# Statistics groups, measuring lead, residual images and opening of a normalise-and-convolve kernel

## The chip, the cores and the metric

One core of a Trainium2 chip. The metric is the device time of the whole program in microseconds, as the median of several runs. The engines are PE (TensorE), DVE (VectorE), ACT (ScalarE), POOL (GpSimd) and SP (SyncE, which here issues DMAs).

## What is computed

160 images of 128 channels and 32x32 pixels are group-normalised (32 groups of 4 channels), convolved with one of five quantised 3x3 weight sets, and added to the input.

```python
def _L0_conv_ref(x, U):
    beta = jnp.max(U); alpha = jnp.min(U)
    s1 = (beta - alpha) / 3.0
    v1 = s1 * _ste_floor(U / s1)
    s2 = s1 / 5.0
    v2 = s2 * _ste_floor((U - v1) / s2)
    w = (v1 + v2).reshape(OUT_CH * N, IN_CH, K, K)
    xb = x.reshape(B // N, N * C, H, W)
    act = jax.lax.conv_general_dilated(xb, w, (1, 1), [(1, 1), (1, 1)], feature_group_count=N)
    return act.reshape(B, C, H, W)
...
x = x + _L0_conv_ref(_gn(x), L0_conv_U)    # _gn: mean and variance over 4 channels and 32x32 pixels
```

The quantisation steps s1 and s2 come from the range of all five weight sets, so no weight is ready before all of U has been read.

## The kernel before

Images are taken set by set, 32 to each of the five weight sets, one image (128 channels on the partitions, 1024 pixels) at a time; they are loaded in pairs. The order of instructions on every engine is written out by hand in `Main.run`: each engine works through its own queue in the order in which the Python code issues, and waits on semaphores.

*Opening* (lines 782 to 899). SP loads the weight sets: the first two in two halves each, the third, image 0, the last two, then image 1 and further images. DVE takes the maximum and the minimum of each piece (`weight_range`, lines 429 and 430). Images 0 and 1 are measured on ACT meanwhile. PE transposes the range across partitions (`over_partitions`, line 443); the matmul for the means of group 0 is issued between this and the matmul that spreads the result (line 448). DVE works out s1, s2, their reciprocals and split parts on 128x1 tiles (`Steps.from_range`), interleaved with the first operations of the first weight column. `lift` is s2 times a constant, and POOL's scales need it (line 241). A weight set is made in three columns of taps (`COLS` = 1, 0, 2), each in some thirteen 128x384 operations on DVE (`quantise`, `floor_div`), turned on PE (line 472) and kept by ACT and POOL (`keep_column`). Idle stretches of PE are filled with `warm_up` matmuls on zeros (line 649). The first three images are convolved directly, column by column.

*Statistics.* An image is measured by two passes on ACT (line 194 for the sum, 201 for the squares) or, for the images in `BY_VECTOR`, by `bn_stats` on DVE (line 184). Images form groups; when all of a group are measured, its statistics take a chain: means on PE (line 210), a copy on ACT (219), four small operations on POOL (221 to 224, tile dv), variances on PE (227), one operation on ACT (233), and `rstd`, `shift`, `twice` on POOL (237 to 246). Means and variances of a group are issued in two successive iterations, within the convs (`on_the_way`).

*The loop* (from line 902), one iteration per image i. PE does `conv(i)`: first the sums of pairs of rows for image i+1 on the bank m (`sums_of_pairs`), then the rest of image i on eo. From image 7 on, odd images are `combined` (differences and sums of rows are formed in float32 by POOL in `outer_rows`, lines 554 and 555, and by DVE in `combine`, then split into vh by ACT, line 576, and vl by DVE, line 582); even ones are normalised by ACT (523, 531) and DVE forms the low part and its row combinations (589, 603 to 606). From image 146 on two of three images are combined. DVE joins the pairs (lines 735 and 737), which frees the bank m; ACT copies one half of it first (725). The operations for the next weight set are taken one at a time out of a generator (`later`), from the fifth image of the first set and the third of the others to the 29th.

*The lead.* Iteration i measures all images below i + min(10 + i//4, 15). So in the iterations 4, 8, 12, 16 and 20 two images are measured, in others one.

*The result.* The scaled sum is either made by ACT (line 754) and added to the image by an accumulating DMA from POOL (773), or, for images that are `by_hand`, added by DVE in one operation (765). In the main part these are i % 8 == 7 from 31 to 151.

Of the kernel before, what the change touches and what calls it, by code (L numbers as in the profile page):

```python
# [33 lines left out]
class Steps:  # L34
# [15 lines left out]
    def from_range(self, extg):  # L50


        nc, col = self.nc, self.col

        def divide_exact(tag, q1, a, m):

            q0, rem = col(tag + "q0"), col(tag + "rem")
            yield nc.vector.tensor_scalar_mul(q0, a, 1.0 / m)
            yield nc.vector.scalar_tensor_tensor(rem, q0, -(m - 1.0), a, ALU.mult, ALU.add)
            yield nc.vector.tensor_sub(rem, rem, q0)  # L60
            yield nc.vector.scalar_tensor_tensor(q1, rem, 1.0 / m, q0, ALU.mult, ALU.add)

        def parts(out, s):

            r, neg, hi, lo = out
            yield nc.vector.tensor_scalar_mul(neg, s, -1.0)
            yield nc.vector.reciprocal(r, s)
            yield nc.vector.tensor_single_scalar(
                hi.bitcast(I32), neg.bitcast(I32), -4096, op=ALU.bitwise_and
            )  # L70
            yield nc.vector.tensor_sub(lo, neg, hi)

        span = col("span")
        yield nc.vector.tensor_reduce(span, extg, AX.X, ALU.add)
        yield from divide_exact("s1", self.s1, span, 3.0)

        of_s1, s2 = parts(self.parts1, self.s1), divide_exact("s2", self.s2, self.s1, 5.0)
        for chain in (s2, of_s1, of_s1, s2, of_s1, s2, s2, of_s1):
            yield next(chain)
        yield nc.vector.tensor_scalar_mul(self.lift, self.s2, LIFT)  # L80
        yield from parts(self.parts2, self.s2)
        self.span, self.big = span, col("big")
        yield nc.vector.tensor_reduce(self.big, extg, AX.X, ALU.max)
# [51 lines left out]
def run(steps):  # L135

    while True:
        try:
            next(steps)
        except StopIteration as end:  # L140
            return end.value
# [170 lines left out]
class Main:  # L312
# [24 lines left out]
    STAT_LEAD = 14  # L337
    LOAD_LEAD = 18
    STEADY = 7
    BY_VECTOR = (8, 10, 11, 14, 19, 24, 29, 34)  # L340
    THIRDS = 146
    EARLY = 8
    FIRST = 3
# [5 lines left out]
    def __init__(self, tc, ctx, keep, x, u, out):  # L349
        nc = self.nc = tc.nc  # L350
        self.imgs, C, self.H, self.W = x.shape
        P = self.P = nc.NUM_PARTITIONS
        assert C == P and self.H * self.W == 1024
        self.per_set = self.imgs // N_SETS
        self.xv = x.rearrange("(b n) c h w -> n c b (h w)", n=N_SETS)
        self.ov = out.rearrange("(b n) c h w -> n c b (h w)", n=N_SETS)
        self.uv = u.rearrange("n (o i k) -> n o i k", o=C, k=TAPS)

        def pool(name, bufs, **kw):
            return ctx.enter_context(tc.tile_pool(name=name, bufs=bufs, **kw))  # L360

        self.const = pool("const", 1)
        self.qpool = pool("quant", 1)
        self.wpool = pool("weights", 2)
        self.upool = pool("u", 1)
        self.xpool = pool("x", 11)
        self.zpool = pool("z", 3)
        self.parts = pool("parts", 5)
        self.rows = pool("rows", 4)
        self.wide = pool("wide", 2)  # L370
        self.wide_parts = pool("wide_parts", 3)
        self.evac = pool("evac", 2)
        self.sums = pool("sums", 3)
        self.unread = pool("unread", 1)
        self.small = pool("small", 3)
        self.ps_eo = pool("ps_eo", 2, space=PSUM)
        ps_m = pool("ps_m", 1, space=PSUM)
        self.ps_stat = pool("ps_stat", 1, space=PSUM)
        self.ps_tr = pool("ps_tr", 1, space=PSUM)
        self.steps = Steps(nc, keep)  # L380

        self.pair = [
            ps_m.tile([P, self.H // 2, self.W], F32, tag=name, name=name) for name in ("m1", "m2")
        ]
        self.chunks, self.z, self.hi, self.v, self.eo, self.m2 = {}, {}, {}, {}, {}, {}
        self.sum = {}
        self.wts = {}
        self.columns = []

        cuts = [0, 2, 4, 8, 12, 16, 20, *range(24, self.imgs + 1, 8)]  # L390
        self.groups = [range(a, b) for a, b in zip(cuts, cuts[1:])]
        self.group_of = {i: k for k, g in enumerate(self.groups) for i in g}
        self.stats = {}
# [28 lines left out]
    def weight_range(self, us):  # L422

        nc, P = self.nc, self.P
        halved = [part for u in us[:2] for part in (u[:, : P // 2], u[:, P // 2 :])]
        pieces = [*halved, *us[2:]]
        ext = self.const.tile([P, 2, len(pieces)], F32, tag="ext", name="ext")
        for k, piece in enumerate(pieces):
            nc.vector.tensor_reduce(ext[:, 0, k : k + 1], piece, AX.XY, ALU.max)
            nc.vector.tensor_reduce(  # L430
                ext[:, 1, k : k + 1], piece, AX.XY, ALU.min, negate=True
            )
        ext1 = self.const.tile([P, 2], F32, tag="ext1", name="ext1")
        nc.vector.tensor_reduce(ext1, ext, AX.X, ALU.max)
        return ext1

    def over_partitions(self, ext1, ident, between):


        nc, P = self.nc, self.P  # L440
        rows = self.ps_tr.tile([1, 2, P], F32, tag="pt", name="rows")
        for k in range(2):
            nc.tensor.transpose(rows[:, k, :], ext1[:, k : k + 1], ident)
        between()
        top = self.const.tile([1, 2], F32, tag="top", name="top")
        nc.vector.tensor_reduce(top, rows, AX.X, ALU.max)
        spread = self.ps_tr.tile([P, 2], F32, tag="pt", name="spread")
        nc.tensor.matmul(spread, self.ones, top, start=True, stop=True)
        return spread
# [44 lines left out]
    def by_vector(self, i):  # L494
        return i in self.BY_VECTOR

    def stats_of(self, k):
        if k not in self.stats:
            self.stats[k] = Statistics(
                self.nc, self.small, self.ps_stat, self.gavg, self.mhalf, len(self.groups[k]),  # L500
                self.steps.lift, k,
            )
        return self.stats[k]

    def measure(self, i, stages=(0, 1)):


        k = self.group_of[i]
        g = self.groups[k]
        st, j, image = self.stats_of(k), i - g.start, self.image(i)  # L510
        if self.by_vector(i):
            st.image(j, image)
            return
        for s in stages:
            junk = self.unread.tile([self.P, 1024], MM, tag="junk", name=f"junk{i}_{s}")
            (st.image_sum, st.image_square)[s](j, image, junk)
# [222 lines left out]
    def by_hand(self, i):  # L739


        if i < self.FIRST or i >= self.imgs - LAST:
            return True
        return i > self.BY_VECTOR[-1] - 4 and i % 8 == 7

    def residual(self, i):

# [34 lines left out]
    def run(self):  # L782
# [4 lines left out]
        for n in range(N_SETS):  # L787
            if n == 0:
                un = self.upool.tile([P, P, TAPS], F32, tag="u", name="u0")
            else:  # L790
                un = self.space(f"range{n}").rearrange("p j e -> p (j e)")[:, : P * TAPS]
                un = un.rearrange("p (i k) -> p i k", k=TAPS)
            half = P // 2 if n < 2 else P
            for c in range(0, P, half):
                nc.sync.dma_start(un[:, c : c + half], self.uv[n][:, c : c + half])
            self.us[n] = un
            if n == 2:
                self.chunks[0] = self.space("xt0")
                nc.sync.dma_start(self.chunks[0][:, 0, :], self.xv[0, :, 0, :])
        nc.sync.dma_start(self.chunks[0][:, 1, :], self.xv[0, :, 1, :])  # L800
        for c in range(1, 6):
            self.load(c, single=c < 2)
        warm = self.const.tile([P, 1], F32, tag="warm", name="warm")
        nc.vector.memset(warm, 0.0)
# [16 lines left out]

        self.ones = self.const.tile([1, P], F32, tag="ones", name="ones")
        nc.vector.memset(self.ones, 1.0)
        ext1 = self.weight_range(list(self.us.values()))
        for i in range(2):
            self.measure(i)
        spread = self.over_partitions(ext1, ident, self.stats_of(0).means)

        def take(steps, count):
            for _ in range(count):  # L830
# [13 lines left out]
        first, second, third = (  # L844
            self.make_column(0, col, by_scalar=col != self.COLS[0]) for col in self.COLS
        )
        for ahead in (11, 2, 1, 1, 1, 1, 1, 1):
            take(chain, ahead)
            take(first, 1)
        run(chain)  # L850
        self.stats[0].deviations()
        measure(0, 2, 3)
        self.stats[0].variances()
        self.stats[0].deviation()
        measure(1, 2)
        self.stats[0].scales()
        take(second, 1)
        measure(1, 3)
        self.stats[1].means()
        self.stats[1].deviations()  # L860
        self.warm_up(14)
        parts(0)
        self.stats[1].variances()
        self.warm_up(8)
        self.stats[1].deviation()
        self.stats[1].scales()
        parts(1)
        run(first)
        self.warm_up(2)
        parts(2)  # L870
        take(second, 2)
        self.low_part(0)
# [29 lines left out]
        for i in range(self.imgs):  # L902
# [27 lines left out]
            else:  # L930
                j = i - 1
                self.conv(i, on_the_way)
            ahead = i + min(10 + i // 4, self.STAT_LEAD + 1)
            to_measure = range(measured, min(self.imgs, ahead))
            measured += len(to_measure)
            if n + 1 < N_SETS:
# [136 lines left out]
```

## Time and profile before

| | us |
|---|---|
| median of 3 runs | 992.03 (991.75 to 992.63) |
| the profiled execution | 991.75 |
| its span, first to last instruction | 989.9 |
| PE busy | 958.1 (97%) |
| DVE busy | 927.7 (94%) |
| ACT busy | 895.0 (90%) |
| POOL busy | 383.7 (39%) |

In the profile's rows an instruction stands with its line in the kernel, its engine, what it writes and reads (tile names without buffer numbers), its shape, and how often it occurs; in a timeline the first column is its start, the second its duration, and a note in brackets tells how long its engine was idle before it and what ended that. PE's matmuls overlap, so a row of 0.38 us is followed by the next after 0.2 us. The granted clock of PE was 0.999 over the span.

### The profile page before, as it was taken

Reading aid. Unit: us, or ns where it says so; the run is one execution under the profiler, and the core shown is the slowest. Engines: PE = TensorE matmul, PEld = TensorE weight load, DVE = VectorE, ACT = ScalarE, POOL = GpSimd, SP = SyncE. Lnnn points to the kernel's source line nnn. Section 1 sums busy time; section 2 is a strip of 40 time slices with the busy share of each in tenths; the row PEclk is TensorE's granted clock in tenths of the full one; section 3 lists DMA queues with packets and bytes.
Section 4 is the critical chain, followed back from the end, with each engine's and each line's share of the span. In section 5 each row is a group of like instructions: output and inputs, shape, how many; then the busy total and the mean of one; then the engine's idle time right before and its main releaser. Section 6 shows DMA issues by size and latency. Waiting matters only on the chain.

```text
span 989.9 us, 16124 instructions
## 1 busy us (share of the span) xinstructions
PE 958.1 (97%) x5938; PEld 578.4 (58%) x5938; DVE 927.7 (94%) x1256; ACT 895.0 (90%) x1224; POOL 383.7 (39%) x565
## 2 busy tenths in 40 slices
PE   2899999999999999999999999999999999999997
PEld 1445655566656666666655666656665666666564
DVE  7999999999999999999999999999999998889995
ACT  5779999899999999999999999999999999998651
POOL 4324563644316253414263443315243424132410
PEclk9999999999999999999999999999999999999999
DMA  9538999999997999899989999997999898987764
GB/s 358 210 107 239 239 241 272 269 265 274 256 306 178 301 249 293 238 278 246 271 217 269 274 279 237 281 283 220 241 278 304 214 301 215 293 229 205 180 178 153
DMA packets 65129, 246.05 MB, mean 249 GB/s; under 512 B 5008, under 2 KB 5008, under 8 KB 65040
## 3 DMA queue, kind: packets, MB, share of 16 engines
q1 hardware_dynamic: 45312, 173.09, 50.2%
q0 software_dynamic: 19728, 71.84, 37.6%
q8 instruction: 48, 0.79, 0.3%
q14 instruction: 41, 0.34, 0.1%
HBM read 89.19 MB, written 83.89 MB: 175 GB/s over the span
## 4 chain that ended last, share of the span: by engine, by line
PE 72%; DVE 13%; ACT 8%; issue 4%; POOL 2%; DMA 0%; DVEq 0%; ACTq 0%; POOLq 0%
PE eo L668 24%; PE m L668 24%; PE eo L629 23%; ACT vh L576 2%; ACT junk L201 2%; ACT sum L754 2%; DVE eo L735 1%; DVE eo L737 1%; DVE v L565 1%; DVE lo L589 1%; POOL v L554 1%; DVE vl L582 1%; ACT m L725 1%; DVE v L568 1%; DVE v L571 1%
## 5 line engine op out<-in xcount | busy, mean ns | idle before, releaser
L668 PEld LDWEIGHTS <-wt 128*128 128x128 f16 x4266 | 417.2, 98 | 234.6 <-issue 6.0
L629 PE MATMUL eo<-hi,wt 128*128 128x496 f16 (+3 forms) x1422 | 339.6, 375 | 1.4 <-ACT wt L485 0.9
L773 POOL DMA_DIRECT2D xt<-sum x137 | 122.4, 899 | 463.6 <-ACT sum L754 448.9
L629 PEld LDWEIGHTS <-wt 128*128 128x128 f16 x1494 | 146.0, 99 | 141.9 <-ACT wt L485 2.3
L582 DVE SCALAR_TENSOR_TENSOR vl<-v,rstd,vh 128x2048 f16<-128x2048 f32 x80 | 188.2, 2353 | 4.1 <-ACT vh L576 4.1
L668 PE MATMUL m<-vh,wt 128*128 128x496 f16 (+1 forms) x480 | 182.2, 380 | 1.8 <-DVE eo L737 1.1
L668 PE MATMUL eo<-vh,wt 128*128 128x248 f16 (+1 forms) x960 | 183.9, 273 | 0.0
L668 PE MATMUL eo<-vl,wt 128*128 128x248 f16 (+1 forms) x960 | 183.9, 273 | 0.0
L668 PE MATMUL m<-vl,wt 128*128 128x496 f16 (+1 forms) x480 | 182.2, 380 | 0.2 <-DVE vl L582 0.2
L194 ACT ACTIVATE junk<-xt 128x1024 f16<-128x1024 f32 x152 | 160.6, 1057 | 15.5 <-DMA xt<-in_x_dram 12.0
L201 ACT ACTIVATE junk<-xt,mv 128x1024 f16<-128x1024 f32 x152 | 173.8, 1144 | 0.1
L576 ACT ACTIVATE vh<-v,rstd 128x2048 f16<-128x2048 f32 x80 | 160.8, 2010 | 2.5 <-POOL v L555 2.0
L754 ACT ACTIVATE sum<-eo 128x1024 f32<-128x1024 f32 x137 | 138.0, 1008 | 15.4 <-PE eo L668 15.3
L735 DVE TENSOR_TENSOR eo<-m,m 128x512 f32<-128x512 f32 x157 | 109.3, 696 | 36.1 <-ACT m L725 29.0
L668 PE MATMUL eo<-rows,wt 128*128 128x256 f16 (+1 forms) x924 | 138.9, 273 | 0.0
L668 PE MATMUL m<-rows,wt 128*128 128x496 f16 (+1 forms) x462 | 113.4, 380 | 0.4
L737 DVE TENSOR_TENSOR eo<-m,m 128x512 f32<-128x512 f32 x157 | 109.5, 697 | 3.6
L725 ACT COPY m<-m 128x512 f32<-128x512 f32 x157 | 90.5, 577 | 18.4 <-PE m L668 18.4
L523 ACT ACTIVATE z<-xt,shift,rstd 128x1024 f32<-128x1024 f32 x80 | 99.8, 1248 | 2.6 <-POOL shift L244 2.6
L589 DVE TENSOR_TENSOR lo<-z,hi 128x1024 f16<-128x1024 f32 x80 | 98.1, 1226 | 0.0
L565 DVE TENSOR_TENSOR v<-xt 128x960 f32<-128x960 f32 x80 | 92.0, 1149 | 0.0
L531 ACT CAST hi<-z 128x1024 f16<-128x1024 f32 x80 | 83.6, 1045 | 2.5
(111 smaller groups left out, 888.1 us busy)
## 6 DMA issues: line engine op xcount, KB each, us to landing
xt<-in_x_dram SPq DMA_DIRECT2D x78, 1024.0 KB, 9.4
out_dram<-xt SPq DMA_DIRECT2D x78, 1024.0 KB, 5.9
xt<-sum POOLq DMA_DIRECT2D x137, 512.0 KB, 6.1
u<-in_L_conv_U_dram SPq DMA_DIRECT2D x4, 576.0 KB, 9.4
xt<-in_x_dram SPq DMA_DIRECT2D x4, 512.0 KB, 9.7
range<-in_L_conv_U_dram SPq DMA_DIRECT2D x3, 576.0 KB, 7.7
out_dram<-xt SPq DMA_DIRECT2D x3, 512.0 KB, 2.8
u<-in_L_conv_U_dram SPq DMA_DIRECT2D x2, 288.0 KB, 3.0
```

The lines of the kernel that those rows point to most:

```text
L194: self.nc.scalar.activation(junk, image, ACTF.Copy, scale=-1.0 / image.shape[1], accum_out=self.mv[:, j, 0:1],)
L201: self.nc.scalar.activation(junk, image, ACTF.Square, bias=self.mv[:, j, 0:1], accum_out=self.mv[:, j, 1:2],)
L565: nc.vector.tensor_sub(v[:, W:last], x[:, : last - W], x[:, 2 * W :])
L576: self.nc.scalar.mul(vh, self.v[i], st.rstd[:, j])
L582: self.nc.vector.scalar_tensor_tensor(vl, self.v[i], st.rstd[:, j], self.hi[i], ALU.mult, ALU.subtract)
L589: self.nc.vector.tensor_sub(lo[:, 1 : self.H + 1, :].rearrange("p h w -> p (h w)"), self.z.pop(i), self.hi[i].rearrange("p h w -> p (h w)"),)
L629: nc.tensor.matmul(self.bank(target, h)[:, r0 - h0 : r1 - h0, c0:c1], self.wts[n, col][:, k, :], tile[:, s0 : s0 + r1 - r0, c0 + dw : c1 + ...
L668: self.nc.tensor.matmul(target[:, :, c0:c1], self.wts[n, col][:, kind, :], source[:, :, c0 + dw : c1 + dw], start=start, stop=stop, skip_g ...
L735: nc.vector.tensor_add(rows[:, :, 0], m1, m2)
L737: nc.vector.tensor_sub(rows[:, :, 1], m1, m2)
L754: nc.scalar.mul(self.sum[i], eo.rearrange("p h r w -> p (h r w)"), 0.5)
L773: self.nc.gpsimd.dma_start(self.image(i), self.sum.pop(i), accum_op=ALU.add)
```

## The change

Five things are changed.

- Groups of statistics: after 0-1 and 2-3, groups of four images up to image 40 (before: up to image 24), and of eight from there.
- The lead of measuring is min(10 + i//8, 15). Two images are measured in iterations 8, 16, 24, 32 and 40.
- `BY_VECTOR` holds 8, 10, 11, 18, 27, 36, 45, 54 instead of 8, 10, 11, 14, 19, 24, 29, 34.
- `by_hand` in the main part takes i % 8 == 3 from 27 to 139, fifteen images, instead of sixteen with i % 8 == 7 from 31 to 151.
- The opening: only the first weight set is loaded and reduced in halves; all weights are loaded ahead of image 0; images 0 and 1 are measured, and the means of group 0 formed, after the range and the chain of steps; s1's parts come ahead of s2; the first column's operations are interleaved with the small ones in another ratio; 14 and 7 warm-up matmuls instead of 14, 8 and 2; the second column's first pass on ACT comes before the squares of image 2, and `high_part(1)` behind the keeping of the first column.

```diff
-        of_s1, s2 = parts(self.parts1, self.s1), divide_exact("s2", self.s2, self.s1, 5.0)
-        for chain in (s2, of_s1, of_s1, s2, of_s1, s2, s2, of_s1):
-            yield next(chain)
+        yield from parts(self.parts1, self.s1)
+        yield from divide_exact("s2", self.s2, self.s1, 5.0)
...
-    BY_VECTOR = (8, 10, 11, 14, 19, 24, 29, 34)
+    BY_VECTOR = (8, 10, 11, 18, 27, 36, 45, 54)
...
-        cuts = [0, 2, 4, 8, 12, 16, 20, *range(24, self.imgs + 1, 8)]
+        cuts = [0, 2, *range(4, 40, 4), *range(40, self.imgs + 1, 8)]
...
-        halved = [part for u in us[:2] for part in (u[:, : P // 2], u[:, P // 2 :])]
-        pieces = [*halved, *us[2:]]
+        pieces = [us[0][:, : P // 2], us[0][:, P // 2 :], *us[1:]]
...
             nc.tensor.transpose(rows[:, k, :], ext1[:, k : k + 1], ident)
-        between()
...
-        return i > self.BY_VECTOR[-1] - 4 and i % 8 == 7
+        return 24 < i < self.imgs - 20 and i % 8 == 3
...
-            half = P // 2 if n < 2 else P
+            half = P // 2 if n == 0 else P
             for c in range(0, P, half):
                 nc.sync.dma_start(un[:, c : c + half], self.uv[n][:, c : c + half])
             self.us[n] = un
-            if n == 2:
-                self.chunks[0] = self.space("xt0")
-                nc.sync.dma_start(self.chunks[0][:, 0, :], self.xv[0, :, 0, :])
-        nc.sync.dma_start(self.chunks[0][:, 1, :], self.xv[0, :, 1, :])
-        for c in range(1, 6):
+        for c in range(6):
             self.load(c, single=c < 2)
...
-        ext1 = self.weight_range(list(self.us.values()))
-        for i in range(2):
-            self.measure(i)
-        spread = self.over_partitions(ext1, ident, self.stats_of(0).means)
+        spread = self.over_partitions(self.weight_range(list(self.us.values())), ident)
...
-        for ahead in (11, 2, 1, 1, 1, 1, 1, 1):
+        for ahead in (8, 1, 1, 1, 1, 1, 3, 1, 1, 1):
             take(chain, ahead)
             take(first, 1)
         run(chain)
+        measure(0, 0, 1)
+        measure(1, 0, 1)
+        self.stats[0].means()
         self.stats[0].deviations()
         measure(0, 2, 3)
         self.stats[0].variances()
         self.stats[0].deviation()
+        take(second, 1)
         measure(1, 2)
         self.stats[0].scales()
-        take(second, 1)
         measure(1, 3)
         self.stats[1].means()
         self.stats[1].deviations()
         self.warm_up(14)
         parts(0)
         self.stats[1].variances()
-        self.warm_up(8)
         self.stats[1].deviation()
         self.stats[1].scales()
-        parts(1)
+        self.normalise(1)
         run(first)
-        self.warm_up(2)
+        self.warm_up(7)
+        self.high_part(1)
         parts(2)
...
-            ahead = i + min(10 + i // 4, self.STAT_LEAD + 1)
+            ahead = i + min(10 + i // 8, self.STAT_LEAD + 1)
```

More of the change, by code (lines that the diff above doesn't have):

```diff
@@ L435, in weight_range, with over_partitions @@
         return ext1
-    def over_partitions(self, ext1, ident, between):
+    def over_partitions(self, ext1, ident):
         nc, P = self.nc, self.P
@@ L495, in by_vector @@
         return i in self.BY_VECTOR
[L497 to L503, printed above, removed]
     def measure(self, i, stages=(0, 1)):
@@ L509, in measure @@
         g = self.groups[k]
-        st, j, image = self.stats_of(k), i - g.start, self.image(i)
+        if k not in self.stats:
+            self.stats[k] = Statistics(
+                self.nc, self.small, self.ps_stat, self.gavg, self.mhalf, len(g),
+                self.steps.lift, k,
+            )
+        st, j, image = self.stats[k], i - g.start, self.image(i)
         if self.by_vector(i):
```

## The prediction

> **What bounds the kernel now.** I read the busy times by stage first, then who waited for whom on PE, then the order of time where PE stood still. Columns of the stages: start and end, length, then busy time (instructions) of PE, PE's weight loads, DVE, ACT, POOL, the granted clock, the DMA share and GB/s.
>
> ```profile
> 0.00:57.00 57.00, 35.12 (x165) 17.10 (x166) 49.56 (x100) 36.75 (x61) 24.52 (x54) 1.00 0.64 247
> 57.00:135.00 78.00, 76.75 (x464) 44.59 (x463) 76.36 (x118) 71.73 (x102) 38.10 (x53) 1.00 0.83 224
> 135.00:234.00 99.00, 97.09 (x604) 58.40 (x603) 94.97 (x133) 95.55 (x134) 49.27 (x62) 1.00 0.98 262
> 234.00:890.00 656.00, 655.87 (x4105) 399.17 (x4104) 621.40 (x814) 635.35 (x871) 246.99 (x360) 1.00 0.93 260
> 890.00:990.00 100.00, 93.27 (x609) 59.19 (x606) 85.47 (x95) 55.60 (x60) 24.85 (x38) 0.99 0.65 180
> ```
>
> From 234 us (image 32 on) PE is busy 655.87 of 656 us: nothing off PE matters there unless it makes PE wait. Before that PE waits; so the change can act in three places: the opening (to 57 us), images 4 to 31 (to 234 us), and the last images.
>
> PE's rate is read from the order of time: a conv begins with its first matmul on m. Undisturbed, a conv of an odd image takes 3.92 us and one of an even image 7.72 (236.21 to 243.93, 243.93 to 247.85). A conv with a group's means or variances in it takes 0.14 more (7.86, 4.06), one that turns a weight column 0.17 more (4.09). Against this the convs of images 14, 18, 23, 24, 25, 29 and 30 are too long by 0.87, 0.71, 0.63, 0.73, 0.26, 0.32 and 0.36 us, 3.9 in all; between 234 and 890 us only three or four by some 0.2; conv 148 by 0.58. Two of them:
>
> ```profile
> 128.99 2.29 POOL L223 TENSOR_TENSOR dv<-dv 128x4 f32<-128x4 f32 x1
> ...
> 131.35 1.90 POOL L224 TENSOR_TENSOR dv<-dv,mv 128x4 f32<-128x4 f32 x1
> ...
> 133.31 0.39 PE L227 MATMUL pg<-dv,gavg 128*128 128x4 f32 x2 [0.61 <-POOL dv L224]
> ```
> ```profile
> 151.91 0.38 PE L668 MATMUL m<-vl,wt 128*128 128x496 f16 x1
> ...
> 152.10 0.68 DVE L737 TENSOR_TENSOR eo<-m,m 128x512 f32<-128x512 f32 x1
> ...
> 152.84 0.38 PE L668 MATMUL m<-vh,wt 128*128 128x512 f16 x1 [0.55 <-DVE eo L737]
> ```
>
> In the first, POOL's chain for a group's variances is late; in the second DVE is late in freeing the bank m. DVE has 97% busy time there and hardly a gap.
>
> The opening is a chain through DVE. It reduces the weights as they land; PE waits for the range, later for the second column:
>
> ```profile
> 7.60 0.75 DVE L429 TENSOR_REDUCE ext<-range 128x1 f32<-128x576 f32 x1
> 8.26 0.75 DVE L430 TENSOR_REDUCE ext<-range 128x1 f32<-128x576 f32 x1
> 8.92 1.35 DVE L429 TENSOR_REDUCE ext<-range 128x1 f32<-128x1152 f32 x1
> ```
> ```profile
> PE rows L443 <- DVE ext L434: 16.9, 1, 16.9
> ...
> PE pt L472 <- DVE k L114: 1.5, 1, 1.5
> ```
>
> **The change, part by part.**
>
> *Second weight set in one transfer, image 0 behind all weights.* DVE reaches the second set at 6.28 us. Its two halves land 4.5 to 5.1 us after their issue at 1.72 and 2.18, so at 6.2 and 7.2. As one transfer it lands at about 7.2, DVE waits 0.9, and two reduces of a whole set (pitch 1.26 each) replace four of a half (0.66): -0.12. The range is ready 0.75 later. Bounds: -0.12 (the one transfer is there at 6.3) to +0.9. I take 0.75. The third set is needed at 9.8 then and lands by 8.7: no second wait.
>
> *Chains of s1 and s2 no longer interleaved.* Before, eleven small operations come ahead of the first large one, now eight; independent ones cost some 0.07 us, dependent ones 0.2, so the first large one starts 0.17 sooner; three more small ones (about 0.1 each) fall between the large ones: +0.13.
>
> *First images measured behind the range.* Images 0 and 1 need four ACT passes of 1.06 to 1.15 us. Image 1 lands at 14.0 as before (the bytes ahead of it are the same), so ACT ends at 17.7, where before it ended at 16.56; but the means matmul now stands behind the spread on PE, 18.0+0.75+0.58, and ngm moves from 17.75 to 19.8. The lift, which POOL's scales wait for, comes after s2, which is now spread between large operations: 21.24 becomes about 24.2. z0 moves from 23.21 to 25.4. PE's 14 warm-up matmuls (0.43 each) begin 2 us later too, and group 1's variances stand behind them: from 26.03 to about 28.5; ve, z, and the keeping of the first column on ACT follow: the first real matmul moves from 29.38 to about 30.9. What hides part of it: PE stands 1.5 us for the second column (k at 38.33) and ACT 3.25 us. Six passes over three images later PE is free at 38.5 instead of 37.0, and k comes at 38.69+0.88 = 39.6. So the second column is set by DVE's chain again, with 0.3 to 1 us of cover left. DVE's own lo's (31.62, 34.12, later by 0.9) need hi 1 and 2, which I get at 32.3 and 34.6: just in time, and 0.3 is lost if they are not. Opening: **+1.1** (0.1 to 1.9). PE is the bound afterwards, so it reaches the end undiminished. Three fewer warm-ups (0.2 each) lie in waits: 0.
>
> *Groups of four to image 40.* 26 groups instead of 24. Each has two matmul pairs at 0.14: 2 x 0.28 = **+0.56** on PE. ACT gets two copies (0.17) and POOL eight small operations more for each. POOL's price is uncertain:
>
> ```profile
> L223 POOL TENSOR_TENSOR dv<-dv x7: 198/198/2287, 65.2 to 253.3; 128x4 f32<-128x4 f32 x4, 128x8 f32<-128x8 f32 x3
> L224 POOL TENSOR_TENSOR dv<-dv,mv x7: 198/203/1899, 65.6 to 253.6; 128x4 f32<-128x4 f32 x4, 128x8 f32<-128x8 f32 x3
> ```
>
> (shortest, median and longest ns). Of the five group chains in convs 6 to 27 one was slow and cost PE 0.87; with two more chains I take 2 x 0.87/5 = **+0.35**, bounds 0 and two whole stalls, 1.74.
>
> The Trainium skill ("SBUF — State Buffer", "Who interferes with whom") says that DVE and GpSimd share one pair of ports as an exclusive lock, so that the later one blocks for the other's whole instruction. The spread of 198 to 2287 ns agrees. Taken strictly it speaks against more POOL chains where DVE has no gaps: both new chains late would be +1.74 instead of +0.35, and the sum 1.4 us higher.
>
> *Lead grows every 8th image; images by vector.* In both kernels an iteration in which two images are measured has one of them on DVE, so ACT's share per iteration stays at one. Those iterations were 4, 8, 12, 16, 20 (images 14, 19, 24, 29, 34) and are 8, 16, 24, 32, 40 (18, 27, 36, 45, 54). An image costs DVE 1.69 us (121.68 to 123.37). So DVE has 1.7 us less behind it from iteration 4 on, 3.4 from 12, 5.1 from 20, and gets them back at 24, 32 and 40. Of the stalls I take the two where PE waits for DVE (0.71 and 0.73) as gone, the two of POOL and ACT (0.87, 0.63) as halved, since these engines are late partly behind DVE, and the last three (0.94) as left: **-2.2**, bounds -3.9 and 0. The 1.69 us at iterations 32 and 40 fall where DVE is busy 95%, and spread over eight images at 5.87 us: I take +0.2, bounds 0 and 1.4 (two stalls like conv 18's).
>
> *Residual on DVE.* It takes DVE 1.22 us and spares ACT a pass of 1.0. It was at images 31, 39, ... 151, sixteen; now 27, 35, ... 139, fifteen. The iterations that carry it move by four against the groups' ends. In the steady part DVE has 5% and ACT 3% free, and I take 0, with -0.4 (the 0.2 stalls vanish) and +2.6 (0.2 at each of 13) as bounds. At the end images 143 and 151 leave DVE for ACT, which is idle there (55.6 of 100 us): conv 148's wait for vl goes, **-0.5**, bounds -0.6 and 0.
>
> Sum: +1.1 +0.56 +0.35 -2.2 +0.2 -0.5 = -0.5. The profiled execution took 991.75 us (span 989.9), the median of the three runs is 0.28 higher. -0.5 gives 991.25, or **991.5** as a median.
>
> **Rivals.**
> *POOL takes DVE's place (slower).* In convs 15, 18, 22, 26 and 29 the four-image chains meet a DVE without gaps and each keeps PE 0.87; the late scales hold up outer_rows and vh, so the old stalls don't shrink either: 1.1+0.56+4.35-0.5 = +5.5 at worst, 997.5; with three of the five late and half the DVE gain, 1.1+0.56+2.6-1.1-0.5 = +2.7, 994.7. It decides from two late chains on. For it: 5.4 us of POOL at 114.57 and 5.3 at 176.15. Against: four of five chains were quick although DVE was busier.
> *The new phase of the residual collides* with the weight steps, 0.2 at each of 13 images on top of the forecast: -0.5+2.6 = +2.1, 994.1. For it: the stages around 340 us have DVE at 29.8 of 30; against: the parity stays.
> *All early stalls go*: 1.1+0.56-3.9-0.6 = -2.8, 989.2. For it: POOL and ACT wait behind DVE; against: convs 29 and 30 lie where DVE gets work back.
> *The second transfer is hidden anyway* and the opening costs 0.1: -1.5, 990.5.
>
> **How the numbers follow.** A change of 0.2%, 2 us, is about what this measurement tells from none. Forecast 0.52, POOL 0.15, phase 0.11, all stalls gone 0.13, transfer hidden 0.09. The forecast's own range, from half the opening's and the stalls' bounds, is 990.0 to 993.5. Faster by over 0.2% is most of "all stalls gone" and little else: 0.12. Slower is POOL, half of the phase and a tail of the forecast: 0.23. The rest, 0.65, is within. The range of 8 in 10 goes from 989.4 to 994.6.
>
> **What would show it.** Right: PE's first wait 17.6 instead of 16.9 with a DVE wait for the second set before it; the first real matmul near 30.9; conv 4 begins about 1.1 later; convs 18 and 24 without a wait; conv 148 at 7.72. Wrong: PE waiting for POOL's dv or ACT's ve in more than one conv; repeated waits at iterations 28, 36, 44 and so on; an opening that moves by more than 1.9, which would mean that PE or ACT, not DVE, sets the second column.

## The result, and the profile after

The changed kernel takes 995.38 us (median of 6 runs, 994.74 to 996.70) against 991.97 for the kernel before: a ratio of 1.0037, 95% interval 1.0024 to 1.0050. It is slower by 3.4 us; the prediction was 991.5, with a range up to 994.6.

The stages of the changed kernel, with columns as before (start and end, length, busy time of PE, PE's weight loads, DVE, ACT, POOL, clock, DMA share, GB/s); the boundary at 234 us is kept so that the rows compare, and conv 32 begins at 236.2 us before and at 237.8 here:

```profile
0.00:57.00 57.00, 33.72 (x161) 16.40 (x162) 49.03 (x98) 36.67 (x61) 27.14 (x54) 1.00 0.64 247
57.00:135.00 78.00, 77.06 (x466) 44.84 (x465) 73.36 (x108) 72.00 (x102) 43.21 (x50) 1.00 0.83 224
135.00:234.00 99.00, 96.22 (x603) 57.99 (x601) 95.38 (x135) 93.87 (x135) 65.83 (x79) 1.00 0.92 255
234.00:310.00 76.00, 74.75 (x473) 45.67 (x470) 72.14 (x101) 72.26 (x98) 30.57 (x39) 1.00 0.96 258
310.00:893.00 583.00, 583.00 (x3647) 354.65 (x3645) 552.65 (x725) 567.07 (x776) 212.59 (x323) 1.00 0.94 261
```

Between 57 and 135 us DVE has 3 us less to do (73.36 against 76.36), and PE is busy for only 0.3 us more (77.06 against 76.75). From 234 to 310 us PE now stands idle for 1.25 us, where before it had no gap. Who PE waited for between 57 and 900 us (total, times, longest), before and after:

```profile
PE m L668 <- DVE eo L737: 1.1, 2, 0.6
PE pg L227 <- POOL dv L224: 0.6, 1, 0.6
PE eo L629 <- DVE eo L737: 0.5, 1, 0.5
PE m L668 <- ACT m L725: 0.5, 1, 0.5
```
```profile
PE m L660 <- DVE eo L729: 2.2, 6, 0.4
PE m L660 <- DVE vl L574: 1.0, 2, 0.7
PE pt L467 <- DVE m L458: 0.8, 1, 0.8
PE eo L621 <- DVE eo L729: 0.5, 1, 0.5
PE pg L225 <- POOL dv L222: 0.2, 1, 0.2
```

Two waits are new: for vl, and for the m of a weight column. Lines have moved by 2 to 8 (L574 is L582 of before, L729 is L737, L458 is L463).

Starts of the convs on PE, compared with before, tell where the time went. Each entry is how much longer that stretch took in the changed kernel's profiled execution:

| stretch | us |
|---|---|
| to the end of conv 3 (opening) | +0.24 |
| convs 4 to 13 | +0.32 |
| convs 14 to 23 | -0.80 |
| convs 24 to 30 | +1.78 |
| convs 31 to 43 | +1.89 |
| convs 44 to 157 | -0.82 |
| sum | +2.6 |

In single convs: conv 12 +0.46; conv 14 -0.87 and conv 15 +0.61; 23 and 24 -0.63 and -0.65; 25 and 26 +0.34 and +1.41; 29 +0.82; 39, 40 and 42 +0.22, +0.56 and +1.10; 49, 81, 113 and 121 some -0.2 each.

The two executions differ by 3.7 us in all. The other 1.1 us lies behind the last instruction on DVE. In the sixteen profiled executions of this study that stretch takes 5.0 to 6.2 us, in kernels of either kind: 5.1 before, 6.1 after.

The new wait for vl, in conv 26 of the changed kernel (from the timeline, start and duration first):

```profile
196.57 1.28 DVE L182 BATCH_NORM_STATS2 st<-xt 128x6 f32<-128x512 f32 x2
197.89 0.21 DVE L184 BATCH_NORM_AGGREGATE both<-st 128x2 f32<-128x12 f32 x1
...
198.26 2.34 DVE L574 SCALAR_TENSOR_TENSOR vl<-v,rstd,vh 128x2048 f16<-128x2048 f32 x1
...
200.66 0.38 PE L660 MATMUL m<-vl,wt 128*128 128x512 f16 x1 [0.68 <-DVE vl L574]
...
201.58 0.69 DVE L729 TENSOR_TENSOR eo<-m,m 128x512 f32<-128x512 f32 x1
...
202.33 0.38 PE L660 MATMUL m<-vh,wt 128*128 128x512 f16 x1 [0.43 <-DVE eo L729]
```

`bn_stats` of image 36, measured in iteration 24, takes DVE from 196.57 to 198.26. vl of image 27 stands behind it, ends at 200.6, and PE waits 0.68 for it. DVE's two operations on the pairs stand behind vl, so PE also waits for the bank m, another 0.43. The same happens at 293.7 us with image 54, measured in iteration 40, where PE waits 0.35 and 0.44.

The kernel before shows how much room there was. Its vl of image 27 ends at 199.60, and PE comes for it at 200.36:

```profile
197.25 2.35 DVE L582 SCALAR_TENSOR_TENSOR vl<-v,rstd,vh 128x2048 f16<-128x2048 f32 x1
...
200.36 0.38 PE L668 MATMUL m<-vl,wt 128*128 128x512 f16 x1
```

That is a margin of 0.76 us, less than the 1.69 that an image by vector takes. The same reading for the three iterations that got one:

| iteration | vl that stands behind | margin before, us | in the changed kernel |
|---|---|---|---|
| 24 | image 27 | 0.76 | PE waits 0.68 |
| 32 | image 35 | 1.94 | no wait, 1.6 left |
| 40 | image 43 | 1.02 | PE waits 0.35 |

PE waits at the two places where the margin was smaller than 1.69, and not at the third.

The 0.78 of convs 39 and 40 has another origin. POOL's scales of the first group of eight (images 40 to 47) come late, ACT waits for them, and the delay reaches PE through the copy of m and the pairs:

```profile
269.75 2.45 POOL L239 TENSOR_SCALAR rstd<-rstd,lift 128x8 f32<-128x8 f32 x1
...
272.52 1.24 ACT L515 ACTIVATE z<-xt,shift,rstd 128x1024 f32<-128x1024 f32 x1 [1.78 <-POOL shift L242]
...
286.69 0.38 PE L660 MATMUL m<-vh,wt 128*128 128x512 f16 x1 [0.41 <-DVE eo L729]
```

The kernel before has the same sequence around its first group of eight (images 24 to 31): POOL's line 241 takes 2.11 us at 172.80, ACT waits 1.80 at 175.23, and PE loses 0.46 and 0.56 at 187.53 and 189.54, in convs 23 and 24. So part of what the change gained there came back at convs 39 and 40.

### The profile page after: what moved, and what is told of

It reads as the page before. It is cut to its first block, busy times and chain, and to the rows that moved or that the text cites. A ratio compares the mean times of both kernels' runs of the same rounds, so it can differ in the third digit from the quotient of the medians.

```text
span 993.6 us, 16152 instructions
## 1 busy us (share of the span) xinstructions
PE 957.6 (96%) x5943; PEld 578.5 (58%) x5943; DVE 925.0 (93%) x1253; ACT 898.6 (90%) x1229; POOL 405.8 (41%) x582
## 4 chain that ended last, share of the span: by engine, by line
PE 72%; ACT 11%; DVE 7%; POOL 5%; issue 4%; DMA 0%; SPq 0%; POOLq 0%; DVEq 0%; ACTq 0%
PE eo L660 24%; PE m L660 23%; PE eo L621 23%; ACT junk L199 3%; ACT vh L568 3%; ACT sum L746 2%; POOL v L546 1%; ACT m L717 1%; POOL rstd L239 1%; DVE v L557 1%; DVE eo L727 1%; DVE eo L729 1%; ACT z L515 1%; ACT junk L192 1%; POOL v L547 1%
## 5 line engine op out<-in xcount | busy, mean ns | idle before, releaser
L765 POOL DMA_DIRECT2D xt<-sum x138 | 126.7, 918 | 445.0 <-ACT sum L746 429.7
L574 DVE SCALAR_TENSOR_TENSOR vl<-v,rstd,vh 128x2048 f16<-128x2048 f32 x80 | 187.8, 2347 | 5.3 <-ACT vh L568 4.7
L729 DVE TENSOR_TENSOR eo<-m,m 128x512 f32<-128x512 f32 x157 | 109.5, 697 | 3.6
```

The lines of the kernel that those rows point to most:

```text
L574: self.nc.vector.scalar_tensor_tensor(vl, self.v[i], st.rstd[:, j], self.hi[i], ALU.mult, ALU.subtract)
L729: nc.vector.tensor_sub(rows[:, :, 1], m1, m2)
L765: self.nc.gpsimd.dma_start(self.image(i), self.sum.pop(i), accum_op=ALU.add)
```

## The experiments

The times are medians in us. "Over before" means the duration of a conv or of a stretch on PE against the profiled execution of the kernel before. In every other profiled execution conv 14's 0.87 is absent (in `more_early` it is 0.33 smaller), and 0.6 to 0.8 stand in convs 15 to 18 in its place. `residual_only` and `residual_from_35` do not differ from the kernel before up to there, so that wait differs between executions and counts for nothing.

### Each part alone

The opening of the changed kernel, with everything else as before (`cuts`, lead, `BY_VECTOR` and `by_hand` restored in the changed kernel):

> The changed kernel's opening alone; groups, lead, images by vector and residual as before. Opening is small (the second set landed at 6.5 us, PE begins image 4 only 0.24 later): the convs start 0.24 later than before and keep that distance, 992.2 us. Rival, the prediction's opening of +1.1: 993.1. Second rival, the shift of 0.24 changes which waits meet in convs 14 to 30: those differ from before by more than 0.3 in sum.

Measured: 993.61 (11 runs, 991.49 to 994.75) against 992.01, ratio 1.0011 (1.0002 to 1.0020). In the profiled execution PE is 2.15 later at image 4, and 1.9 at the last image; the sum over convs 14 to 157 differs by 0.3. So the opening does not disturb the loop, but its own cost isn't the 0.24 that I expected. It follows one landing, as DVE's timeline in this execution shows:

```profile
5.80 0.74 DVE L427 TENSOR_REDUCE ext<-u 128x1 f32<-128x576 f32 x1
8.51 1.35 DVE L426 TENSOR_REDUCE ext<-range 128x1 f32<-128x1152 f32 x1 [1.97 <-DMA range<-in_L_conv_U_dram]
```

The second set as one transfer landed by 6.5, 7.4 and 8.5 us in the changed kernel, in `between_weights` and here, DVE's last reduction of the range began 0.16, 1.01 and 2.11 us later than before, and PE came to image 4 later by 0.24, 1.45 and 2.15 us. These are three executions; the landings of the unprofiled ones are not known. With two halves DVE had the first half to work on, and image 4 began within 0.37 of before in every execution.

Groups, lead and images by vector alone (the residual images, whose first one in the kernel before follows from `BY_VECTOR`, are kept from 31 on):

```diff
-    BY_VECTOR = (8, 10, 11, 14, 19, 24, 29, 34)
+    BY_VECTOR = (8, 10, 11, 18, 27, 36, 45, 54)
-        cuts = [0, 2, 4, 8, 12, 16, 20, *range(24, self.imgs + 1, 8)]
+        cuts = [0, 2, *range(4, 40, 4), *range(40, self.imgs + 1, 8)]
-            ahead = i + min(10 + i // 4, self.STAT_LEAD + 1)
+            ahead = i + min(10 + i // 8, self.STAT_LEAD + 1)
```

> Groups, lead and images by vector of the changed kernel; opening and residual as before. If DVE's bn_stats ahead of vl, at iterations 24 and 40 where weight steps are under way, is what costs PE: waits for vl and for the pairs stand in convs 25, 26 (1.9 us) and 42 (1.1 us), the early gain of about 1.5 stays, two groups add 0.56, and the time is about 994. If the moved residual is the cause instead, these waits are gone and the time is 991.5 or less.

Measured: 998.07, ratio 1.0061 (1.0047 to 1.0075), worse than the whole change. The waits for vl are there, in three convs instead of two, and convs 39 to 42 take 4.5 over before instead of 1.9. Here residual images are i % 8 == 7, so image 39 has its residual in iteration 40, the very iteration in which image 54 is measured:

```profile
293.18 1.21 DVE L765 SCALAR_TENSOR_TENSOR xt<-eo,xt 128x1024 f32<-128x1024 f32 x1
...
296.40 1.28 DVE L184 BATCH_NORM_STATS2 st<-xt 128x6 f32<-128x512 f32 x2
...
298.08 2.34 DVE L582 SCALAR_TENSOR_TENSOR vl<-v,rstd,vh 128x2048 f16<-128x2048 f32 x1
...
300.48 0.38 PE L668 MATMUL m<-vl,wt 128*128 128x512 f16 x1 [0.81 <-DVE vl L582]
```

So the moved residual relieves the moved lead.

The residual alone:

```diff
-        return i > self.BY_VECTOR[-1] - 4 and i % 8 == 7
+        return 24 < i < self.imgs - 20 and i % 8 == 3
```

> The kernel before with only the residual images moved to i % 8 == 3 from 27 to 139. If bn_stats is the main cost: a wait of PE for DVE's m in conv 29 (some 0.8) and a late ACT copy of m in conv 40 (some 0.6), less the stalls of 0.2 at convs 49, 81, 113 and 122, about +0.6, 992.6. If the residual's phase is the main cost: +2.5 or more, 994.5, with waits in convs 25, 26 and 42.

Measured: 992.48 against 992.01, ratio 1.0006 (0.9997 to 1.0015). Conv 29 is 1.34 longer, convs 49, 81, 113 and 121 together 0.8 shorter; conv 40 is unchanged. In iteration 28 the generator of weight steps is run to its end, and the residual of image 27 now stands ahead of these steps on DVE; PE, which turns the column, waits:

```profile
218.17 1.22 DVE L765 SCALAR_TENSOR_TENSOR xt<-eo,xt 128x1024 f32<-128x1024 f32 x1
...
223.14 0.56 DVE L463 SCALAR_TENSOR_TENSOR m<-k,k 128x384 f16<-128x384 f16 x1
...
223.76 0.35 PE L472 MATMUL pt<-ident,m 128*128 128x128 f16 x3 [1.07 <-DVE m L463]
```

### Where bn_stats stands

Lead steps moved to iterations 30, 32 and 34, between two weight sets:

```diff
-    BY_VECTOR = (8, 10, 11, 18, 27, 36, 45, 54)
+    BY_VECTOR = (8, 10, 11, 18, 27, 42, 45, 48)
-            ahead = i + min(10 + i // 8, self.STAT_LEAD + 1)
+            ahead = i + 10 + sum(i >= at for at in (8, 16, 30, 32, 34))
```

> The changed kernel with the last three lead steps at iterations 30, 32, 34 (images 42, 45, 48 by vector) in place of 24, 32, 40, so that bn_stats falls where no weight step is due. If bn_stats beside weight steps is the cost: the waits in convs 25, 26 and 42 go (3.0 us), the new places cost 0 to 0.5 each, 992.5 to 993.5. If the residual or the groups' chains are the cause, these waits stay and the time is 995.

Measured: 995.59, ratio 1.0033 (1.0021 to 1.0045). The waits for vl are gone and convs 40 and 42 are as before, but conv 26 keeps 0.46, and convs 32, 36 and 37 are 2.1 longer. Of the sum of convs 24 to 43 only 0.7 of 3.7 us is won, and the opening took 1.45 in this execution. PE waits there for DVE's pairs. The expectation was missed; that three steps within five iterations are too dense is my reading, which no run tests.

The changed kernel with the opening of before, the base for the runs that follow:

> The changed kernel with the opening of before. If the opening's cost is the landing of the second set alone (the changed opening cost PE 0.24, 1.45 and 2.15 us in three executions), the loop's waits stay as in the changed kernel: conv 25 and 26 together 1.8 over before, conv 29 0.8, convs 39 to 42 1.9, and the time is 1.6 below the changed kernel's, 993.8. If the moved opening shifts what meets in the loop, these sums differ by more than 0.5.

Measured: 995.16, ratio 1.0031 (1.0019 to 1.0043). PE reaches image 4 with 0.03 of difference, and the loop is the changed kernel's conv by conv: +1.8 in convs 24 to 30 and +1.9 in 31 to 43. The 1.6 us that I expected from the opening's removal are not in the median; 0.2 are. The changed kernel's six runs spread over 2 us, these over 0.5, which fits landings that differ from run to run; they were not traced.

The three late images measured by ACT, so that DVE has no bn_stats in iterations 24, 32 and 40 (`BY_VECTOR = (8, 10, 11, 18, 27)`):

> As old_opening, but images 36, 45 and 54 are measured by ACT like all others, so iterations 24, 32 and 40 give ACT two images and DVE no bn_stats. If bn_stats on DVE ahead of vl is the cause, PE waits for vl no more in convs 25, 26 and 42 (-1.8 and -1.1); if the two images in one iteration are the cause whatever engine measures them, 2.2 us more on ACT give waits for the copy of m or for vh of at least the same size, 1 to 2 us at each of the three.

Measured: 998.07 (one run). The waits for vl are gone, and larger ones have come: conv 25 takes 1.99 over before, conv 41 1.78, and PE waits for ACT, which has two images' passes to do ahead of its copy of m:

```profile
PE m L668 <- ACT m L725: 3.0, 2, 1.6
PE m L668 <- DVE eo L737: 2.8, 8, 0.6
PE pt L472 <- DVE m L463: 1.1, 1, 1.1
```

At iterations 24 and 40 neither engine has room for a second image; DVE is the cheaper of the two (convs 24 to 43 take 3.7 over before with DVE, 6.8 with ACT).

More work on DVE in the iterations where the kernel before had its bn_stats (results unused):

```diff
                 measure(0, *by_vector)
+                if i in (4, 12, 20):
+                    more = self.const.tile([P, 2, 8], F32, tag="more", name=f"more{i}")
+                    for h in range(2):
+                        nc.vector.bn_stats(
+                            more[:, h, :6], self.image(i + 9)[:, h * 512 : h * 512 + 512]
+                        )
...
```

> As old_opening, with one image's bn_stats work more on DVE (unused results) at the end of iterations 4, 12 and 20. If DVE has time there that nothing else can use, the convs up to 18 lose less than 0.4 in sum, and only the one at iteration 20 costs PE, 0.5 to 1.4 in convs 21 to 24. If DVE's work counts wherever it stands, 1 us or more is lost by conv 18 and some 4 us in all.

Measured: 994.46 (one run); PE's last image begins 2.70 later than before, against 2.68 in `old_opening` (net of the opening 2.77 and 2.65). Three images' bn_stats work, 5.1 us of DVE, costs 0.1. In iteration 20:

```profile
170.78 1.28 DVE L1019 BATCH_NORM_STATS2 more<-xt 128x6 f32<-128x512 f32 x2
...
172.47 2.35 DVE L582 SCALAR_TENSOR_TENSOR vl<-v,rstd,vh 128x2048 f16<-128x2048 f32 x1
...
175.38 0.38 PE L668 MATMUL m<-vl,wt 128*128 128x512 f16 x1
```

vl ends at 174.8 and PE takes it at 175.38 without a wait: 0.6 us are left even with the additional work. In iteration 24 of the changed kernel vl came too late by 0.7.

bn_stats of images 36, 45 and 54 one iteration later, behind the vl:

```diff
-                measure(0, *by_vector)
+                measure(0, *held)
+                held = by_vector if i in (24, 32, 40) else []
+                if not held:
+                    measure(0, *by_vector)
```

> As old_opening, but the bn_stats of images 36, 45 and 54 stand one iteration later on DVE (at the end of 25, 33, 41), so behind the vl that they held up and ahead of a low part. If it is the place that costs, because vl is due before 1.69 us more fit in: PE's waits for vl in convs 26 and 42 go and what follows them, 2 to 2.5 us in all, 992.8. If DVE has no time in these iterations wherever the work stands, waits of about the same sum come one conv later, 995.

Measured: 993.99, ratio 1.0013 (1.0004 to 1.0022), against 1.0031 for `old_opening`, which was measured beside other runs of the kernel before. PE waits for vl nowhere; convs 26, 39, 40 and 42 are as before. Part of it comes back: conv 29 goes from +0.82 to +1.69, convs 27 and 37 take 0.56 and 0.48 more. PE waits there for DVE's pairs and for the m of a weight column. So 3.3 us go and 1.9 come back: net of the opening the PE order is 1.4 us shorter than in `old_opening`. The place alone explains somewhat less than half of these waits; for the rest DVE has no time one iteration later either.

### Groups, lead and residual taken apart

Groups of four to image 40, with the old lead and nothing else:

> The kernel before with groups of four up to image 40 and nothing else. The two groups more cost PE 4 x 0.14 = 0.56. If the gain of the changed kernel in convs 23 and 24 (0.63 and 0.68 below before) comes from the smaller group, whose chain on POOL no longer meets them, it is here too and the PE order ends 0.7 earlier than before; if it comes from less bn_stats on DVE, it is absent and the kernel ends 0.6 later.

Measured: 995.12 (one run), 3.0 later on PE net of the opening, not 0.6. Convs 23 and 24 together take 0.43 less, not 1.3. Convs 26, 28, 29 and 33 take 3.1 more, and conv 73 0.55; PE waits for DVE's pairs, for DVE's m and for ACT's copy, not for POOL. The trace shows where most of it comes from. POOL's scales of a four-image group, `rstd` with 4.71 us at 190.93 and `twice` with 2.31 at 196.62, stand ahead of the accumulating DMA, which POOL issues at 200.67 instead of 195.40. The store that waits for it goes out at 205.36 instead of 202.33, the load behind the store at 205.91 instead of 202.88, and ACT has to wait for the image:

```profile
218.00 1.06 ACT L194 ACTIVATE junk<-xt 128x1024 f16<-128x1024 f32 x1 [3.35 <-DMA xt<-in_x_dram]
```

DVE then stands 2.42 us for ACT's copy of m, and PE for both, in convs 28 and 29. So POOL's chain costs PE without PE ever waiting for POOL. It is one execution.

The lead and the images by vector of before, in `old_opening`; groups and residual stay changed:

> As old_opening, but the lead and the images by vector as in the kernel before: what stays of the change is the groups of four to image 40 and the moved residual. If the lead steps at iterations 24 and 40 are the main cost, convs 25, 26 and 39 to 42 lose nothing more against before (3.7 us less), while conv 29 and what the groups alone cost (3.0 in the run with groups only, of it 2.5 in convs 26 to 29) stay: 993.5 to 995. If the groups' chains are the cause of those waits, convs 39 to 42 stay slow.

Measured: 992.06 against 991.86, ratio 0.9999 (0.9990 to 1.0009). Convs 39 to 42 are as before, convs 25 and 26 take 0.1 more in sum. Conv 29 keeps 1.58 and conv 37 0.57; convs 44 to 157 gain 0.8. Beside the moved residual the groups are cheaper than with the old one, although ACT waits for a late image here too (3.41 at 217.82). With `old_opening` at 1.0031, the lead with its images by vector is what made the loop slower. Its size is less certain: the ratios differ by 0.0032, some 3 us, the PE order of the two profiled executions by 1.6 (2.65 against 1.06 net of the opening), and the execution profiled here was among the two longest of its ten runs.

The first residual image 35 instead of 27, in `old_opening`:

```diff
-        return 24 < i < self.imgs - 20 and i % 8 == 3
+        return 30 < i < self.imgs - 20 and i % 8 == 3
```

> As old_opening, with the first residual image 35 instead of 27, so that DVE has no residual in iteration 28, where the last steps of the weight column stand. If the residual there makes the column late, conv 29 is back to the time of before (0.82 less) and the total 0.8 lower, 994.3; if the column is late by the bn_stats of iteration 24 alone, nothing changes.

Measured: 993.10, ratio 1.0010 (1.0000 to 1.0019). Conv 29 is 0.18 below before, so the residual in iteration 28 is what made the column late. Convs 39 and 40 are also as before, which I had not expected: ACT still waits 1.60 for POOL's scales at 271.07, but no more for POOL's v after that, and the delay does not reach PE. Why POOL is quicker there was not tested. Conv 26 and conv 42 keep their 1.41 and 1.08.

### What is faster than both

The kernel before with residual images from 35 (`30 < i < self.imgs - 20 and i % 8 == 3`):

> The kernel before with residual images i % 8 == 3 from 35 to 139. The wait of PE for DVE's m in conv 29 (1.3 over before with image 27) is gone, the small stalls at convs 49, 81, 113 and 122 stay away: -0.9 against before, 991.1. If ACT misses the help of the first residuals, convs 31 to 36 lose 0.5 or more.

Measured: 991.37 against 991.92, ratio 0.9996 (0.9987 to 1.0005). Conv 29 is as before, convs 49, 81, 113 and 121 gain 0.8; PE's last image begins 0.94 earlier net of the opening. The times alone don't tell it from no change.

With one group of four more:

```diff
-        cuts = [0, 2, 4, 8, 12, 16, 20, *range(24, self.imgs + 1, 8)]
+        cuts = [0, 2, *range(4, 32, 4), *range(32, self.imgs + 1, 8)]
-        return i > self.BY_VECTOR[-1] - 4 and i % 8 == 7
+        return 30 < i < self.imgs - 20 and i % 8 == 3
```

> The kernel before with groups of four up to image 32 (one group more: +0.28) and residual images i % 8 == 3 from 35 to 139 (0.8 less at convs 49, 81, 113 and 121). If the smaller group takes away the waits of convs 23 and 24, -1.3: 990.2. If not, 991.5.

Measured: 990.85 (11 runs, 990.75 to 991.96) against 992.69, ratio 0.9981 (0.9972 to 0.9990): faster than both. Conv 23 takes 0.30 less, conv 24 is unchanged; PE's order is 1.2 us shorter net of the opening, so part of the measured gain lies in the runs of before beside it, whose median was higher than in the other comparisons (992.0, 991.9 and 991.9).

### The second set in halves

The changed kernel with the second set again in two transfers and four reduces:

```diff
-        pieces = [us[0][:, : P // 2], us[0][:, P // 2 :], *us[1:]]
+        halved = [part for u in us[:2] for part in (u[:, : P // 2], u[:, P // 2 :])]
+        pieces = [*halved, *us[2:]]
-            half = P // 2 if n == 0 else P
+            half = P // 2 if n < 2 else P
```

> The changed kernel with the second weight set again loaded and reduced in two halves. If the landing of the one transfer sets how late the changed opening is (6.5, 7.4 and 8.5 us gave 0.24, 1.45 and 2.15), PE reaches image 4 within 0.4 of the kernel before in this execution, and the times are 0 to 1 below the changed kernel's with less spread. If the order of measuring is what delays it, 1 us or more stays.

Measured: 994.55 (10 runs, 994.05 to 994.80), ratio 1.0019 (1.0010 to 1.0028). Image 4 begins 0.04 later than before. The spread is 0.75 us, against 1.96 in the six runs of the changed kernel. So in this execution only the one transfer costs; measuring the first images later, the other order of s1 and s2 and the fewer warm-ups are hidden together. Nothing is left of the cover: PE, which stood 1.49 us for the second column before, now waits 1.43 for ACT's high part of image 2 and turns the column without a wait.

## Why the prediction was wrong

**The step that failed** is the one on lead and images by vector: "-2.2, bounds -3.9 and 0" for the early convs, and "I take +0.2, bounds 0 and 1.4" for the work that returns. It treated DVE's time as one account: 1.7, 3.4, 5.1 us "less behind it", so that waits for DVE would go. `more_early` puts the whole 5.1 us back into iterations 4, 12 and 20 and loses 0.1; DVE had room there, although its busy share was 97%. Convs 23 and 24 did gain 1.3, but keep that gain with the work put back, so it came from the lead and the groups and not from DVE's load: POOL's chain of the first eight-image group no longer stands there, and costs 0.78 at convs 39 and 40 instead. The wait in conv 24, which I counted as DVE's, belonged to that chain: DVE itself had stood 1.35 us for ACT's copy of m. Conv 18, counted as gone, gained 0.14. And the returning work cost 1.8 in convs 25 and 26 and 1.1 in conv 42 where I had 0.2. I priced only iterations 32 and 40, and put the price of iteration 24 nowhere. At 32 it was nothing; 24 and 40 together cost 2.9, twice the bound that I had given for two places. What decides is not a busy share but the margin of one operation: how long ahead of PE vl is ready. The trace of the kernel before had it: 0.76 us at iteration 24 and 1.02 at 40, against 1.69 us of work, and 1.94 at 32. `late_by_scalar` shows that the other engine would have paid more. In all, the forecast gave the lead -2.0 us (-2.2 and +0.2); between `lead_back` and `old_opening` it costs 1.6 on PE in the profiled executions and some 3 by the ratios.

**The residual** was taken as 0 with bounds -0.4 and +2.6. The small gain at four convs (-0.8) was real and larger than the bound; the loss sat at a single image, 27, through the weight steps in iteration 28, and not at thirteen. The loss stayed inside the bound, but for a reason that the prediction did not have. The -0.5 for the end was wrong: conv 148 still takes 0.59 over its undisturbed 7.72, and PE still waits there for vl, with images 143 and 151 gone from DVE.

**Groups**: the 0.14 for each matmul pair is right (convs 8, 11, 17, 21 and others are longer by exactly that, and others shorter). PE's waits for POOL's dv went from 0.6 to 0.2 in sum, so the +0.35 for late chains was not needed, and the strict reading of the Trainium skill's port rule ("SBUF — State Buffer", "Who interferes with whom") that I set beside it, 1.74, even less. But PE's waits for POOL are not the whole price. POOL's busy time grew by 22 us for 17 instructions (405.8 against 383.7), and a slow chain reaches PE by two other paths, which no step had: through ACT's wait for the scales (convs 39 and 40 of the changed kernel), and through a late accumulating DMA, store and load (`groups_only`, where the groups cost 3.0).

**The opening** was right about the transfer and unsettled in its size. When the one transfer lands late, DVE waits and the range is late, and image 4 with it; the later first images are hidden (`second_halved`: 0.04). The +1.1 is the landing at 7.2 us; 6.5, 7.4 and 8.5 were measured. In the changed kernel's profiled execution it was +0.24 (PE's first wait 17.1 instead of the 17.6 foreseen, the first real matmul at 29.70 instead of 30.9), in `opening_only` 2.15, above the bound of 1.9. The path was partly wrong: the prediction had DVE's chain set the second column with 0.3 to 1 us of cover left. In the changed kernel k is ready at 38.76 and PE, held up for 1.42 us by ACT's high part of image 2, comes for it at 38.92, so the cover is used up and PE no longer waits for k.

**The rivals.** "POOL takes DVE's place" gave 994.7, near the measured time. Its price, PE waiting for POOL's dv in several convs, is refuted: PE waited less for POOL than before. Its remark that late scales hold up ACT holds at one place, for 0.78 us of the 4.5 that convs 25, 26, 29, 39, 40 and 42 lost. "The new phase of the residual collides" is right for one image only, and in the whole the phase helps: without it the lead costs 998.07.

## What to carry to other kernels

Price a moved piece of work by the margin of the operation that will stand behind it on its engine, at the very place where it goes, not by the engine's busy share over a stretch: at 97% busy 1.7 us were free in one iteration and cost 1.8 in another four iterations on. List every place where work returns and give each a price. Two additions to one engine, here residual and statistics, should be checked for meeting in the same iteration before either is tried alone.

## What the runs showed of the hardware

The landing of one transfer of 576 KB, third in its queue, varied from 6.5 to 8.5 us between three executions with the same loads ahead of it. DVE's last reduction of the range and the start of image 4 moved with it (0.16 and 0.24, 1.01 and 1.45, 2.11 and 2.15 us later than before). With the set in two halves the start of image 4 lay between 0.07 earlier and 0.37 later than in the kernel before, in twelve executions of as many kernels.

One and the same small POOL operation took several microseconds more or less in the profile: `rstd` on 128x4 4.71 us in `groups_only` at 190.93, and 2.52 at 214.73. At the first of these places the chain delayed an accumulating DMA by 5 us, and with it a store and a load by 3.
